# A mixer of two Mamba passes on one core: ScalarE scales the projected rows, VectorE adds them in one piece, and the queues of a unit are put in another order

## The chip, the core and the metric

The kernel runs on one core of a Trainium2 chip. The core has five engines that work from queues of their own: TensorE (PE, matrix products and transposes, results in PSUM), VectorE (DVE), ScalarE (ACT), GpSimd (POOL) and SyncE (SP, which here only starts DMAs). An engine takes its instructions strictly in the order in which they stand in its queue. An instruction that needs the result of another engine waits for a semaphore, and everything behind it in that queue waits too. The metric is the device time of one launch in microseconds (us), lower is better.

## What is computed

Input is x of shape (8, 32, 32, 128) in float32: 8 sequences of 1024 tokens with 128 channels. Layer 0 is a group norm with attention. Layer 1 adds the mixer to the tokens, and then a spectral filter. The change lies in the mixer:

```python
def _mamba3(x, in_proj, conv_w, conv_b, A_log, dt_bias, D, norm_w, out_proj):
    zxbcdt = x @ in_proj
    z, xbc, dt = jnp.split(zxbcdt, [D_INNER, D_INNER + CONV_DIM], axis=-1)
    xp = jnp.pad(xbc, ((0, 0), (K - 1, 0), (0, 0)))
    conv = sum((xp[:, i:i + l, :] * conv_w[:, i] for i in range(K))) + conv_b
    xbc = jax.nn.silu(conv)
    xh, Bm, Cm = jnp.split(xbc, [D_INNER, D_INNER + D_STATE], axis=-1)
    dt = jax.nn.softplus(dt + dt_bias)
    A = -jnp.exp(A_log)
    y = _ssd(xh, dt, A, Bm, Cm) + xh * D[None, None, :, None]
    yg = y.reshape(b, l, D_INNER) * jax.nn.silu(z)
    yn = yg * jax.lax.rsqrt(jnp.mean(yg * yg, -1, keepdims=True) + EPS) * norm_w
    return yn @ out_proj
...
t = t + _L1_attn_ref(_ln_t(t), ...)   # forward pass + pass over the reversed tokens
```

D_INNER is 256 (four heads of 64), D_STATE 64, K = 4 taps. `_ssd` works in chunks of 64 tokens: inside a chunk, C B^T is multiplied by a triangle of decays exp(segsum) and applied to x dt; each chunk also leaves a state, the states are passed on from chunk to chunk with a decay, and C, weighed with the decay since the chunk's start, reads them.

## The kernel before, in words

**Units.** The mixer works on 16 units (b, d): sequence b = 0 to 7, direction d = 0 (forward) and d = 1 (backward, on the same layout with mirrored taps and triangles). One turn of the loop at L1187 is one unit, some 36 us; two make a sequence. The loop overlaps three units: while unit `u` has its scan, `following` is projected and convolved, and `last` is gated, normed and projected out. `after_it`, two units ahead, only gets its decays. `fresh` is the next sequence, whose normed tokens are turned (`turn_tokens`) and whose step sizes (softplus, `steps`) are computed while d = 0 runs.

**Order.** No scheduler chooses here: `tc.manual_schedule` (L1152) keeps the instructions of every engine in the order in which the Python code issues them. So the order of the calls in the loop is the order of all queues.

**Names of a unit**, by what the profile calls them:

- `cums`, `dsum`, `cs`, `rest`, `dec`: cumulated log decays and what is made of them (`add_decays` L792, `turn_decays` L807, `take_decays` L813, which also sends them through memory, `cd`, so that rows come back spread over partitions as `lm` and `ec`).
- `lm`: from a row of cumulated decays to the triangle of a chunk: GpSimd subtracts (`from_row`, L846), ScalarE takes relu and then exp of minus it in two halves each (`between`, L852), VectorE multiplies by `gm` (`weigh_decays`, L1034 with the operation on L1038, called C's weighing below, since `gm` is C B^T). `ec`: GpSimd multiplies by C (`weigh_start`, L857).
- `pp`, `xp`, `xs`: x projected (PSUM), copied with a pad (ScalarE, `copy_x`), convolved per half of 128 channels: one tap with the bias on ScalarE (`first_tap`, L893), three taps on VectorE (`convolve`, L901), silu on ScalarE (`activate_x`, L906).
- `pz`, `zs`: the gate projected, and its silu (L914). `pb`, `bt`, `ct`: B and C, projected and convolved at once by TensorE (L923), and their silu.
- `sx`, `xdt`, `xdd`: x turned by TensorE (L952) and multiplied by dt (L955), then by the decay to the chunk's end (`decayed_x`).
- `sb`, `bg` = (`bk`, `gm`): B turned, and C B^T (L969), copied by ScalarE; `gm` then gets its triangle mask.
- `pst`, `state`, `moved`: the chunks' states (`chunk_states`, L990) and their passing on, 29 VectorE instructions (`pass_states`, L1007, the "states" of the text below).
- `sy`: eight steps of output products in two halves (`outputs`, L1042).
- `y`: `sy` plus D x (`add_x`, L1072), times `zs` (`gate`, L1087, which also squares into `zs`, L1090).
- `misc`, `sums`, `rms_v`, `rms`: sums of the squares over channels on TensorE (`square_sums`, L1109), copied, turned (`turn_sums`, L1123), scaled by VectorE (L1125) and raised to the power -1/2 by GpSimd (L1127).
- `spo`: `y` times the output weights (`project_out`), 128 tokens by 128 channels for each of eight blocks j. `add_up` (L1131) does X[j] = spo[j] * rms[j] + X[j], eight times. After d = 1, X goes out to memory (`xd`) and comes back in another layout (`reload`, L1140) for the spectral stage.

**Buffers that tie the units.** The tags `spo`, `misc`, `pst` and `sy` come from one PSUM pool (`ps_s`), `sx`, `sb`, `px`, `pp`, `pz`, `pb`, `pd` and `pdec` from another (`ps_w`). Each pool has two buffers, handed out in turn in the order of the calls. A new tile waits until the readers of the one in its place are done. So the first of the two tiles of `pst` waits for whoever reads `spo`.

**Two orders written by hand** in addition: `behind` puts `from_row` and `weigh_start`, both on GpSimd, after a chosen VectorE instruction (the last tap of a half so far).

**Norm of later sequences.** In d = 1 the layer norm of sequence b + 2 is taken: `normalize` (L442, statistics on VectorE, power on GpSimd) and `normalized` (eight ScalarE instructions `ln_x`, L458, in two groups of four).

## Time and profile before

| what | us |
|---|---|
| three runs | 1492.85, 1494.98, 1498.38 |
| profiled execution: its run, its span | 1490.8, 1489.0 |
| granted TensorE clock in it | 0.974 |

Busy time of each engine in stretches of the profiled span:

| stretch, us | what runs | PE | DVE | ACT | POOL |
|---|---|---|---|---|---|
| 0 to 465 | attention | 438.68 | 366.44 | 297.33 | 237.31 |
| 465 to 610 | mixer, b = 0 and 1 | 125.62 | 113.95 | 96.42 | 42.62 |
| 683 to 757 | b = 3 | 66.77 | 61.21 | 49.57 | 23.46 |
| 757 to 828 | b = 4 | 65.07 | 60.72 | 49.05 | 23.21 |
| 828 to 900 | b = 5 | 65.37 | 61.45 | 49.99 | 23.63 |
| 900 to 964 | b = 6 | 57.36 | 55.00 | 42.95 | 20.70 |
| 964 to 1042 | b = 7 | 66.02 | 59.38 | 45.29 | 24.00 |
| 1042 to 1165 | end of the mixer, spectral part | 102.60 | 63.08 | 48.79 | 64.47 |
| 1165 to 1430 | spectral part | 259.11 | 197.07 | 148.35 | 32.97 |
| 1430 to 1489 | end | 39.37 | 25.01 | 1.33 | 0 |

The stretches of the mixer are cut at round times near the units' borders, so they aren't equally long. A good mark of a unit is the copy of its first state (L1013): these stand at 500.16, 538.02, 574.40, 610.03, 646.39, 682.72, 719.22, 756.71, 793.29, 828.21, 864.55, 899.76, 936.25, 973.75, 1008.42 and 1040.82 us. Their distance is what a unit costs. The last addition to X begins at 1067.52 and the spectral part's first copy at 1069.83.

How to read the lines of instructions further on: start in us, duration in us, engine, line of the code, operation, output and inputs by their names, shape, x how many instructions the line stands for, and in brackets the idle time of the engine just before it, with the engine, tile and line that ended it. "issue" is idle time in which the engine waited for nothing that the profile shows. In a row of a group (it begins with the line and engine) the two numbers behind the bar are the busy time and the mean ns of one. In a row of a window come: its borders, length, busy time of PE, PE's weight load, DVE, ACT and POOL with the number of instructions, the granted clock, the DMAs' busy share and GB/s.

### The profile page before, as it was taken

To read this page: it belongs to the slowest core of one execution; us is meant where nothing else is said; L and a number is where in the kernel's file an instruction comes from. 1 tells how busy PE (TensorE), PEld (TensorE's weight loads), DVE (VectorE), ACT (ScalarE), POOL (GpSimd) and SP (SyncE) were. 2 spreads that over 40 slices of the span, in tenths; PEclk is the share of its full clock that TensorE was granted. 3 is DMA by queue.
4 is the path that set the end of the run, shared out by engine and by line. 5 is a ranking of instruction groups with operands and counts; after the bars stand their busy time and mean duration, and the time that the engine had idled before them with its cause. 6 is when DMAs were issued, how large, how long until landed. Compare 5 with 4: busy or idle time off the path is not lost.

```text
span 1489.0 us, 45246 instructions
## 1 busy us (share of the span) xinstructions
PE 1351.5 (91%) x19782; PEld 843.7 (57%) x19782; DVE 1124.6 (76%) x2250; ACT 878.9 (59%) x1293; POOL 516.0 (35%) x510
## 2 busy tenths in 40 slices
PE   5999999999998789998989898997599899999977
PEld 2233333333334456565656566655489888899963
DVE  5688888788766788888888888877645577777745
ACT  2666666766765676767676767564255455555520
POOL 3326966876212232323232333232276111111100
PEclk8999999999999999999999999999899999999989
DMA  7101111110002334343424343431259322322258
GB/s 183 31 1 30 43 36 36 50 50 8 8 1 58 76 77 112 77 108 75 109 66 112 78 106 72 101 72 43 71 171 243 105 68 67 88 72 75 68 150 310
DMA packets 139383, 123.09 MB, mean 83 GB/s; under 512 B 44809, under 2 KB 118153, under 8 KB 135081
## 3 DMA queue, kind: packets, MB, share of 16 engines
q1 hardware_dynamic: 137064, 115.93, 30.3%
q10 hardware_dynamic: 2112, 4.19, 0.7%
q8 instruction: 157, 2.57, 0.7%
q14 instruction: 50, 0.40, 0.1%
HBM read 78.15 MB, written 34.08 MB: 75 GB/s over the span
## 4 chain that ended last, share of the span: by engine, by line
PE 60%; DVE 14%; issue 10%; ACT 9%; POOL 4%; DMA 2%; DVEq 0%; SPq 0%; ACTq 0%; POOLq 0%
PE pg L1407 10%; PE pt L626 9%; PE py L1441 8%; PE po L647 7%; DVE state L1016 4%; PE pd L667 4%; PE sy L1064 3%; PE pb L923 2%; POOL ec L859 2%; PE pf L1325 2%; PE pz L868 2%; ACT ln_x L458 2%; POOL rms L1127 1%; DVE y L1078 1%; PE pz L1520 1%
## 5 line engine op out<-in xcount | busy, mean ns | idle before, releaser
L631 ACT ACTIVATE pr<-pt 128x1024 f32<-128x1024 f32 x256 | 248.0, 1021 | 117.3 <-PE pt L626 115.9
L656 DVE TENSOR_TENSOR two<-pr,pr 128x1024 f32<-128x1024 f32 x128 | 162.8, 1312 | 19.4 <-ACT pr L631 18.5
L1418 DVE COPY gs<-pg 128x512 f32<-128x512 f32 x256 | 158.8, 684 | 19.8 <-PE pg L1407 15.1
L1420 ACT COPY gs<-pg 128x512 f32<-128x512 f32 x256 | 132.7, 604 | 68.9 <-PE pg L1407 53.1
L626 PE MATMUL pt<-q,k 32*128 32x512 f32 x1024 | 160.7, 658 | 7.0 <-ACT pr L631 4.5
L1407 PE MATMUL pg<-taps,mst 32*128 32x128 f32 x4096 | 148.3, 283 | 6.7 <-ACT gs L1420 3.1
L1407 PEld LDWEIGHTS pg<-taps,mst 32*128 32x128 f32 x4096 | 135.0, 190 | 20.2 <-issue 14.7
L647 PE MATMUL po<-pr,v 128*32 128x512 f32 x1024 | 141.1, 609 | 0.0
L901 DVE SCALAR_TENSOR_TENSOR xs<-xp,cw,xs 128x1024 f32<-128x1024 f32 x96 | 123.1, 1283 | 16.3 <-ACT xs L893 12.8
L859 POOL TENSOR_TENSOR ec<-ec,ct 128x2048 f32<-128x2048 f32 x16 | 72.7, 4541 | 163.5 <-issue 104.0
L1441 PE MATMUL py<-gs,u 128*32 128x128 f32 (+1 forms) x4096 | 127.8, 277 | 0.0
L923 PE MATMUL pb<-bxt,wbc 128*128 128x512 f32 x256 | 117.3, 612 | 7.2 <-ACT zs L914 7.2
L1441 PEld LDWEIGHTS py<-gs,u 128*32 128x32 f32 (+1 forms) x4096 | 112.0, 141 | 7.2
L1127 POOL TENSOR_TENSOR rms<-rms_v,mhalf 128x8 f32<-128x8 f32 x16 | 39.5, 2466 | 206.8 <-DVE rms_v L1125 206.8
L1430 POOL TENSOR_SCALAR u<-u 128x512 f32<-128x512 f32 x16 | 23.9, 1496 | 231.1 <-DMA u<-ud 158.9
L626 PEld LDWEIGHTS pt<-q,k 32*128 32x128 f32 x1024 | 47.7, 188 | 86.6 <-issue 33.5
L1016 DVE SCALAR_TENSOR_TENSOR state<-state,dec,pst 128x64 f32<-128x64 f32 x448 | 87.4, 275 | 1.3
L923 PEld LDWEIGHTS pb<-bxt,wbc 128*128 128x128 f32 x256 | 48.3, 193 | 66.2 <-issue 57.9
L1064 PE MATMUL sy<-lm,xdt 64*64 64x64 f32 x2048 | 67.5, 227 | 16.8 <-DVE lm L1038 9.5
L1064 PEld LDWEIGHTS sy<-lm,xdt 64*64 64x64 f32 x2048 | 62.2, 137 | 28.3 <-issue 28.1
L647 PEld LDWEIGHTS po<-pr,v 128*32 128x32 f32 x1024 | 28.1, 110 | 88.4 <-issue 84.5
L458 ACT ACTIVATE ln_x<-X,b_shift,ln_r 128x128 f32<-128x128 f32 x128 | 51.8, 481 | 37.2 <-DVE b_shift L453 37.2
(277 smaller groups left out, 2771.2 us busy)
## 6 DMA issues: line engine op xcount, KB each, us to landing
lm<-cd SPq DMA_DIRECT2D x32, 512.0 KB
ec<-cd SPq DMA_DIRECT2D x32, 512.0 KB
ud<-sp SPq DMA_DIRECT2D x8, 1024.0 KB
u<-ud SPq DMA_DIRECT2D x32, 256.0 KB
yd<-sums SPq DMA_DIRECT2D x32, 256.0 KB
moved<-state SPq DMA_DIRECT2D x48, 128.0 KB
yt<-yd SPq DMA_DIRECT2D x6, 1024.0 KB
X<-in_x SPq DMA_DIRECT2D x8, 512.0 KB
```

The lines of the kernel that those rows point to most:

```text
L626: nc.tensor.matmul(pt[:, i, :], lhsT=k[rows, j * P : (j + 1) * P], rhs=q[rows, cols], start=True, stop=True)
L631: nc.scalar.activation(pr[:, 2 * g : 2 * g + 2, :].rearrange("p i t -> p (i t)"), pt.rearrange("p i t -> p (i t)"), AF.Exp, scale=SCALE,)
L647: nc.tensor.matmul(po[rows, :], lhsT=vs[b][:, j, rows], rhs=pr[:, h, :], start=(j == 0), stop=(j == NT - 1))
L656: nc.vector.tensor_tensor(two, sums["pr"][:, 2 * g : 2 * g + 2, :], pr[:, 2 * g : 2 * g + 2, :], ALU.add)
L901: u.convolved = nc.vector.scalar_tensor_tensor(acc, xp[:, at : at + T], cw[u.d][:, n, i : i + 1], acc, ALU.mult, ALU.add)
L923: nc.tensor.matmul(u.pb[:, i * 512 : (i + 1) * 512], lhsT=wbc[u.d][:, k, :], rhs=xt[:, at : at + 512], start=(k == 0), stop=(k == KC - 1),)
L1016: nc.vector.scalar_tensor_tensor(u.state[:, k, h, :], u.state[:, k - 1, h, :], u.dec[:, c, h, j : j + 1], u.pst[c][:, j, h, :], ALU.mult, ...
L1064: nc.tensor.matmul(u.py[c][h * HP : (h + 1) * HP, r, j, :], lhsT=left, rhs=right, start=(kind == 0), stop=(kind == 1 or k is None),)
L1407: nc.tensor.matmul(pts[g][:, e, :], lhsT=mst[rows, n * 4 + e, :], rhs=taps[rows, cols].rearrange("p f q m i -> p (f q m i)"), start=True, ...
L1418: nc.vector.tensor_copy(to, frm)
L1420: nc.scalar.copy(to, frm)
L1441: nc.tensor.matmul(py[t * 32 : t * 32 + 32 - 16 * m, q // 2, :], lhsT=u[:, i, m:, :, :, q * FC + f].rearrange("p k b i -> p (k b i)"), rhs ...
```

## The change

- `add_up` is replaced by two steps. `scale_rows`: eight ScalarE activations (Identity with a per-row scale `rms`) from `spo` into the first half of `y`. `add_rows`: one VectorE addition of the 128x1024 result to X, at the end of the unit, behind the second half of the outputs. The store of X follows it; `reload` comes one unit later (`stored`).
- `turn_x` comes before `add_x(last)`: the turned x and `xdt` stand ahead of `y` on VectorE.
- `between(u, Exp)` comes right after `take_decays`, ahead of `bg` on ScalarE, for both directions.
- Both gates, and so both squares, come before the second half of x is projected and copied; `first_tap(following, 0)` comes after `end(last)` instead of before the gates, `first_tap(following, 1)` after the gate's projections.
- `add_decays(after_it)` of d = 1 comes before `decayed_x`, `turn_decays` of it right after `end(last)`.
- `weigh_decays(u, 0)` comes right after `decayed_x`, the second half before the taps of `following`; both stood after `pass_states`.
- `end` has the sums turned between blocks 4 to 5 and 6 to 7 of `spo`, instead of behind the taps of `following`.
- Taps 0 and 1 of half 0 stay before the states, tap 2 and silu of half 0 go behind them. So `from_row` and `weigh_start` follow other instructions.
- In `steps`, `sp_u` (1 + exp) comes after the pause in the generator, so that `weigh_decays(u, 1)` and two taps stand ahead of it.
- In `normalize`, the power on GpSimd may be issued later than the statistics, and is then put behind a tap of `following`.

The arithmetic stays the same apart from where the product with `rms` is rounded.

```diff
@@ -124,10 +124,12 @@
     mhalf = filled("mhalf", [P, 1], -0.5)
     quarter = filled("quarter", [P, 1], 0.25)
+    begun = []
+
     def rsqrt(pool, src, n, scale, eps, name):
         t = pool.tile([P, n], F32, tag=name + "_v", name=name + "_v")
-        nc.gpsimd.tensor_scalar(t, src, scale, eps, ALU.mult, ALU.add)
+        begun.append(nc.gpsimd.tensor_scalar(t, src, scale, eps, ALU.mult, ALU.add))
         r = pool.tile([P, n], F32, tag=name, name=name)
         nc.gpsimd.tensor_tensor(r, t, mhalf.to_broadcast([P, n]), ALU.pow)
         return r
@@ -439,14 +441,14 @@
         nc.vector.tensor_reduce(far[0:1, 0:1], pf, AX.X, ALU.add)
         nc.vector.tensor_copy(bad, far[0:1, 0:1])
-    def normalize(pool, b):
+    def normalize(pool, b, later=False):
         st = pool.tile([P, NT, 6], F32, tag="ln_st", name=f"b_st{b}")
         mv = pool.tile([P, NT, 2], F32, tag="ln_mv", name=f"b_mv{b}")
         for j in range(NT):
             nc.vector.bn_stats(st[:, j, :], X[b][:, j, :])
         for j in range(NT):
             nc.vector.bn_aggr(mv[:, j, :], st[:, j, :])
-        return mv, rsqrt(pool, mv[:, :, 1], NT, 1.0, 1e-5, "ln_r")
+        return mv, None if later else rsqrt(pool, mv[:, :, 1], NT, 1.0, 1e-5, "ln_r")
     def normalized(b, pool, mv, rstd, wide=None):
         shift = pool.tile([P, NT], F32, tag="ln_s", name=f"b_shift{b}")
@@ -501,9 +503,9 @@
         nc.vector.tensor_scalar(e, v, -1.0, None, ALU.mult)
         nc.vector.tensor_tensor(e, e, v, ALU.min)
         nc.scalar.activation(e, e, AF.Exp)
+        yield
         u = small("sp_u")
         nc.vector.tensor_scalar(u, e, 1.0, None, ALU.add)
-        yield
         lg = small("sp_l")
         nc.scalar.activation(lg, u, AF.Ln)
         yield
@@ -1089,10 +1091,10 @@
             nc.vector.tensor_tensor(u.y[:, n, :], u.y[:, n, :], u.zs[:, n, :], ALU.mult)
             nc.scalar.activation(u.zs[:, n, :], u.y[:, n, :], AF.Square)
-        def project_out(u, half):
-            if half == 0:
+        def project_out(u, js):
+            if js[0] == 0:
                 u.po = wide_psum(ps_s, f"spo{u.tag}").rearrange("p (j e) -> p j e", j=NT)
-            for j in range(4 * half, 4 * half + 4):
+            for j in js:
                 for n in range(2):
                     nc.tensor.matmul(
                         u.po[:, j, :],
@@ -1128,12 +1130,15 @@
                 u.rstd, v.rearrange("p q k -> p (q k)"), mhalf.to_broadcast([P, NT]), ALU.pow
             )
-        def add_up(u):
+        def scale_rows(u):
+
+            u.rows = u.y[:, 0, :].rearrange("p (j c) -> p j c", j=NT)
+            for j in range(NT):
+                nc.scalar.activation(u.rows[:, j, :], u.po[:, j, :], AF.Identity, scale=u.rstd[:, j : j + 1])
+
+        def add_rows(u):
             x = X[u.b]
-            for j in range(NT):
-                nc.vector.scalar_tensor_tensor(
-                    x[:, j, :], u.po[:, j, :], u.rstd[:, j : j + 1], x[:, j, :], ALU.mult, ALU.add
-                )
+            nc.vector.tensor_tensor(x, x, u.rows, ALU.add)
             if u.d == 1:
                 nc.sync.dma_start(xd[u.b].rearrange("(j p) c -> p j c", p=P), x)
@@ -1159,10 +1164,12 @@
         def end(u):
-            project_out(u, 0)
-            u.misc = wide_psum(ps_s, f"misc{u.tag}")
-            square_sums(u, u.misc)
-            project_out(u, 1)
+            project_out(u, range(4))
+            misc = wide_psum(ps_s, f"misc{u.tag}")
+            square_sums(u, misc)
+            project_out(u, range(4, 6))
+            turn_sums(u, misc)
+            project_out(u, range(6, 8))
         add_decays(first)
         turn_decays(first)
@@ -1183,80 +1190,83 @@
         activate_bc(first)
         compare_denominators(most, least, wide_psum(ps_w, "pf")[0:1, :2])
-        last = None
+        last = stored = None
         for at, u in enumerate(units):
             following = units[at + 1] if at + 1 < len(units) else None
             after_it = units[at + 2] if at + 2 < len(units) else None
             fresh = u.b + 1 if u.d == 0 and u.b + 1 < B else 0
+            early_decays = after_it and u.d == 1
             if following and u.d == 1:
                 turn_decays(following)
             if at == 0:
                 between(u, AF.Relu, 1.0)
             if following:
                 take_decays(following)
+            between(u, AF.Exp, -1.0)
+            turn_x(u)
+            weigh_start(u, u.convolved)
             if last:
                 add_x(last)
-            turn_x(u)
-            weigh_start(u, u.convolved)
             turn_b(u)
             if fresh:
                 turn_tokens(fresh, seqs[fresh], wide_psum(ps_w, f"px{fresh}"))
             if following:
-                take_x(following, 0)
+                project_x(following, 0)
+                copy_x(following, 0)
             if last:
                 gate(last, 0)
+                gate(last, 1)
             if following:
                 project_x(following, 1)
-            if last:
-                gate(last, 1)
-            if following:
                 copy_x(following, 1)
+            if early_decays:
+                add_decays(after_it)
             decayed_x(u)
+            weigh_decays(u, 0)
             if last:
                 end(last)
+            if early_decays:
+                turn_decays(after_it)
             if following:
-                first_tap(following, 1)
-                convolve(following, 0, range(pad - 1))
+                first_tap(following, 0)
             if last:
-                turn_sums(last, last.misc)
-            early_decays = after_it and u.d == 1
-            if early_decays:
-                add_decays(after_it)
-            else:
-                between(u, AF.Exp, -1.0)
-            if following:
-                convolve(following, 0, range(pad - 1, pad))
+                scale_rows(last)
+            b = u.b + 2 if following else 0
+            norm = None
+            if u.d == 1 and b < B:
+                norm = normalize(bridge, b, later=True)
             going = iter(())
             if fresh:
                 going = steps(fresh, seqs[fresh], wide_psum(ps_w, f"pd{fresh}"))
                 next(going)
-                next(going)
-            project_z(u, 0)
-            if early_decays:
-                turn_decays(after_it)
-                between(u, AF.Exp, -1.0)
-            activate_z(u, 0)
-            project_z(u, 1)
-            activate_z(u, 1)
+            weigh_decays(u, 1)
             if following:
-                activate_x(following, 0)
-            if last:
-                add_up(last)
+                convolve(following, 0, range(pad - 1))
             next(going, None)
-            b = u.b + 2 if following else 0
-            norm = normalize(bridge, b) if u.d == 1 and b < B else None
+            for n in range(2):
+                project_z(u, n)
+                activate_z(u, n)
+            if following:
+                first_tap(following, 1)
+            if norm:
+                mv = norm[0]
+                norm = mv, rsqrt(bridge, mv[:, :, 1], NT, 1.0, 1e-5, "ln_r")
+                if following:
+                    behind(begun[-1], following.convolved, "beside the states")
             if following:
                 from_row(following, following.convolved)
             chunk_states(u)
             pass_states(u)
+            next(going, None)
             norming = normalized(b, bridge, *norm) if norm else iter(())
             next(norming, None)
-            if last and last.d == 1:
-                reload(last)
-            weigh_decays(u, 0)
-            weigh_decays(u, 1)
+            if stored:
+                reload(stored)
+            stored = None
             if following:
+                convolve(following, 0, range(pad - 1, pad))
+                activate_x(following, 0)
                 between(following, AF.Relu, 1.0)
                 project_bc(following)
                 activate_bc(following)
@@ -1268,13 +1278,16 @@
                 activate_x(following, 1)
             next(norming, None)
             outputs(u, 1)
+            if last:
+                add_rows(last)
+                stored = last if last.d else None
             last = u
         add_x(last)
         for n in range(2):
             gate(last, n)
         end(last)
-        turn_sums(last, last.misc)
-        add_up(last)
+        scale_rows(last)
+        add_rows(last)
         reload(last)
     early.close()
```

## The prediction

> **What bounds the kernel now.** I read the page's busy shares first, then a window of one sequence in the mixer, then the instructions in order of time on each engine in that window.
>
> ```profile
> PE 1351.5 (91%) x19782; PEld 843.7 (57%) x19782; DVE 1124.6 (76%) x2250; ACT 878.9 (59%) x1293; POOL 516.0 (35%) x510
> ```
>
> TensorE is busy 91% over all, but the change touches only the mixer (about 478 to 1070 us), so the stretch to read is one sequence there, two units (d = 0 and d = 1):
>
> ```profile
> 610.00:683.00 73.00, 65.50 (x990) 43.85 (x990) 61.33 (x140) 49.86 (x72) 23.66 (x16) 1.00 0.38 88
> ```
>
> Of 73.00 us TensorE is busy 65.50, VectorE 61.33, ScalarE 49.86. Neither of the first two is full: they wait for one another in turn. The gain open to any new order is what TensorE idles, some 7 us a sequence. TensorE's own lines say for whom it waits (start, duration, last the idle time and its releaser):
>
> ```profile
> 610.37 7.11 PE L923 MATMUL pb<-bxt,wbc 128*128 128x512 f32 x16 [0.44 <-ACT zs L914]
> ...
> 623.26 1.86 PE L952 MATMUL sx<-ident,xs 128*128 128x128 f32 x15 [0.53 <-ACT xs L906]
> 626.36 1.15 PE L969 MATMUL sb<-ident,bt 64*64 64x64 f32 x32 [1.25 <-DVE xdt L955]
> ...
> 635.81 0.64 PE L1109 MATMUL misc<-zs,ones 128*32 128x256 f32 x8 [0.20 <-ACT zs L1090]
> ```
> ```profile
> 664.25 1.15 PE L969 MATMUL sb<-ident,bt 64*64 64x64 f32 x32 [1.87 <-DVE xdt L955]
> ...
> 672.52 0.64 PE L1109 MATMUL misc<-zs,ones 128*32 128x256 f32 x8 [0.20 <-ACT zs L1090]
> ...
> 678.74 1.99 PE L868 MATMUL pz<-bxt,win 128*128 128x512 f32 x4 [0.28 <-ACT cs L811]
> ```
>
> With 0.40 before sy (653.64, for C's weighing L1038), 0.43 before the second pb (683.07) and 0.3 inside pst (643.81 to 646.11, where 1.98 is its length, for the X sums L1134) these waits make 0.44 + 0.53 + 1.25 + 0.20 + 0.30 + 0.40 + 1.87 + 0.20 + 0.28 + 0.43 = 5.90 us. The other 1.95 us (0.78 and 1.17, both inside sy) have the releaser "issue": nothing that the change moves ends them, and I leave them.
>
> VectorE and GpSimd:
>
> ```profile
> 639.11 0.17 DVE L1125 TENSOR_SCALAR rms_v<-misc 128x8 f32<-128x8 f32 x1 [2.54 <-PE misc L1123]
> ...
> 642.00 2.16 DVE L1134 SCALAR_TENSOR_TENSOR X<-spo,rms,X 128x128 f32<-128x128 f32 x8 [0.39 <-POOL rms L1127]
> ```
> ```profile
> 493.42 3.62 POOL L846 TENSOR_TENSOR lm<-cs,lm 128x2048 f32<-128x2048 f32 x1 [8.88 <-DVE xs L901]
> ...
> 1034.92 1.63 POOL L1127 TENSOR_TENSOR rms<-rms_v,mhalf 128x8 f32<-128x8 f32 x1 [9.60 <-DVE rms_v L1125]
> ```
> ```profile
> 493.51 3.58 DVE L501 TENSOR_SCALAR sp_e<-sp_v 128x64 f32<-128x64 f32 x1
> ```
>
> **The Trainium skill.** "SBUF — State Buffer", section "Who interferes with whom", says that VectorE and GpSimd share a port pair: a VectorE operation with two SBUF inputs, or a one-source one in a two-port mode (tensor_scalar among them), and a GpSimd operation that reads SBUF shut each other out; the first to start holds it. The trace agrees: sp_e (0.20 us elsewhere) took 3.58 from 493.51 because L846 had begun at 493.42. The power rms takes 1.63 alone and 2.54 at the median, where a tap ran first. "ScalarE: Activation LUTs", section "What ACT_TABLE_LOAD costs", prices a per-row pointer operand at about 93 ns and the overlap of neighbouring activations at about 93 ns. The rows below agree.
>
> ```profile
> L458 ACT ACTIVATE ln_x<-X,b_shift,ln_r 128x128 f32<-128x128 f32 x128 | 51.8, 481 | 37.2 <-DVE b_shift L453 37.2
> ...
> L893 ACT ACTIVATE xs<-xp,cb,cw 128x1024 f32<-128x1024 f32 x32 | 39.8, 1242 | 0.6
> L906 ACT ACTIVATE xs<-xs 128x1024 f32<-128x1024 f32 x32 | 33.9, 1058 | 13.8 <-DVE xs L901 13.7
> ...
> L1456 ACT COPY half<-py 128x128 f32<-128x128 f32 x64 | 17.0, 265 | 66.0 <-ACT gs L1420 36.1 <-issue 22.1 <-PE py L1441 7.9
> ```
>
> L893 has two pointers where L906 has none: 184 ns more, 92 each. Eight ln_x in a row take 3.19 us, 0.39 apart, so 0.09 of 0.481 overlap.
>
> **The change, part by part.** I walk the queues of one sequence with these durations, start to start: tap 1.27; 128x1024 tensor_tensor 1.13; y 0.66; states 5.7; silu 0.97; relu or exp of half lm 0.95; bg, bxt 1.0; bt and ct together 2.78; table 1.29; sx 0.95 a half; sb 2.0; px 1.15; pp or pz 1.8 each; spo 1.87 for eight products' half; pst 1.98; pb 7.05; a hand-over of about 0.14 (0.18 from TensorE).
>
> *Scaled rows.* Removed: eight L1134, 2.08 us on VectorE. Added: one 128x1024 addition, 1.13 us, after the last tap, hidden while TensorE finishes sy. Added on ScalarE: eight 128x128 activations from PSUM with one pointer: L1456's 265 + 92 - 93 overlap = 0.27 us, 2.2 together. Bounds: 0.20 (nothing for the pointer) to 0.39 (ln_x's spacing). I take 0.27. They stand before zs in ScalarE's queue, and pst waits for them instead of L1134.
>
> *xdt before y.* xdt's first half now follows half of sx at once: 0.95 + 0.18 + 1.13 + 0.14 = 2.40 against sx's 1.90, so sb waits 0.50 instead of 1.25 and 1.87. Gain 2.1 a sequence.
>
> *Squares before the second xp copy, C weighed early, decays added before spo, pst no longer behind L1134.* The waits 0.20, 0.20, 0.40 and 0.28 go, as the work now ends over 0.5 us ahead. pst's 0.30 becomes 0.18 in d = 1: first_tap ends, 8 x 0.27 = 2.2 follow, while spo's last quarter and pz (4.6) run. Gain 1.2.
>
> *Exp of lm moved ahead of bg.* Where ln_x's second half lies in front (d = 0), ScalarE needs from silu to bg's end 1.56 + 1.29 + 0.69 + 1.91 + 1.0 = 6.45, plus 0.14. TensorE reaches pp after 0.14 + 0.95 + 0.18 + 1.13 + 0.14 + 2.0 + 1.15 = 5.69. New wait 0.90; none in d = 1, where bg waits for sb as before.
>
> *sp_u (L505) behind two taps and one weighing (d = 0).* From the end of pd: 0.18, softplus head 0.68, weighing 1.13, taps 2.54, sp_u 0.18, 0.14, then on ScalarE ln 0.27, table 1.29, zs 0.92, 0.14 = 7.5. TensorE has pz 3.6 and pst 2.0 meanwhile, so pb waits 1.9, where it waited for nothing here. In d = 1 the wait for zs stays at some 0.23 (0.43).
>
> *Last tap of half 0 behind the states, so silu of half 0 stands between ln_x and relu.* In d = 1, from the states' start: 5.7 + 0.2 + 1.56 + 0.97 + 1.90 + 2.78 + 0.97 + 0.14 = 14.2 until sx may start; TensorE is there after 0.17 + 7.05 + 5.4 = 12.6. Wait 1.56 instead of 0.53. In d = 0 it just fits.
>
> Sum of waits after: 0.50 + 0.50 + 0.90 + 1.89 + 0.23 + 0.18 + 1.56 = 5.76, against 5.90. Per sequence -0.1; over six, -0.8.
>
> *Ends of the mixer.* In unit 0 sp_e is no longer behind L846. bg ends at 486.9 (two exps later), pp 490.6, pd 492.3, pz 495.9, pst 497.9: the states start 2.2 us before the old 500.16. In (6,1) and (7,0) nothing but one weighing and two taps (3.7 us, all two-input) follows rms_v on VectorE, so the power has to wait for all three instead of one; pst of the next steps slips by about 1.5 each, +3. At the very end 2.2 + 1.1 replace 2.16, less two of spo's rows: +0.6. DMAs: the xd store leaves at the unit's end, before the cd store, whose exps come 4 us later; reload goes one unit later, past the moved copies and well before the transform. Both cost nothing: SP's queue is waiting there anyway.
>
> Total: -0.8 - 2.2 + 3 + 0.6 = +0.6 us on the profiled span of 1489.0. The runs shown have 1490.8 to 1498.4 with median 1494.98; I forecast **1495 us**, no change. About 0.5% (7.5 us) is what a measurement of this kernel can tell from no change.
>
> **Rivals.**
> - *Faster.* The removed waits (3.3 us a sequence) are all plain, the added ones (c. 3.2: bg, zs, silu) are small differences of long ScalarE chains. If these chains run half a microsecond shorter each, or the issue gaps of sy fall into the new waits, half of the gain stays: 1.7 x 7 = 12 us: 1483. For it: VectorE ends with 2 to 3 us of slack in each unit. Against: ScalarE's busy time rises to about 54 of 72.
> - *Slower by ScalarE's queue.* If the eight activations cost ln_x's 0.39, d = 1 gains 1.0 us of wait on pst, and both last units too: +8, 1503; with 0.5, +15.
> - *Slower by the port.* sp_u is a tensor_scalar directly behind the tap that releases L846's operation. If L846 gets the port first, sp_u is held 3.6 us, and ln, zs and pb with it: 7 x 3.4 = +24, 1519. It decides when sp_e's exponential ends after the second tap (now 2.6 us before it), or if the hand-over to GpSimd beats the next VectorE issue; at 640.39 sp_v followed a tap without a gap and L846 began 0.08 after its tap, so I doubt it.
> - *Not what it says*: the queues are kept in written order, so it is done.
>
> **Numbers.** Forecast 0.45, faster 0.30, ScalarE's queue 0.15, port 0.10. So faster 0.30, same 0.45, slower 0.25. Range 1482 to 1513: the likeliest alone 1488 to 1502, the rest takes in 12 us to the fast side and ScalarE at 0.5; the port's case is left out.
>
> **What would show it.** sb's wait near 0.5; L1134 gone, eight activations 0.27 apart; pb waiting near 1.9 for zs in d = 0; sx waiting 1.5 for silu in d = 1; sp_u 0.2 long. It is wrong if sp_u shows 3.6, if a sequence in mid-mixer is not 71 to 74 us, or if pst waits over 1 us for the scaled rows.

## The result, and the profile after

The changed kernel takes 1474.16 us (median of four runs, 1471.66 to 1474.91), the kernel before on the same chip 1496.49: a ratio of 0.9851, interval 0.9827 to 0.9875. The forecast was no change, 1495 us in 1482 to 1513. The kernel became faster by 22 us, and the time lies outside the range.

The profiled spans are 1489.0 and 1469.9 us, 19.1 apart. Cut at marks that both traces have, the difference lies here (us; "first state" is the copy L1013, now L1015):

| stretch | before | after | difference | forecast |
|---|---|---|---|---|
| start to the mixer's first sx | 477.43 | 474.26 | -3.17 | 0 |
| first sx to unit 0's first state | 22.73 | 20.95 | -1.78 | -2.2 |
| unit 0 to unit 12 (six sequences) | 436.09 | 431.58 | -4.51 | -0.8 |
| unit 12 to unit 15 | 104.57 | 103.10 | -1.47 | +3 |
| unit 15 to the end of the last addition to X | 28.86 | 29.58 | +0.72 | +0.6 |
| from there to the end | 419.32 | 410.43 | -8.89 | 0 |

The first row is an execution's own scatter: the instructions there are the same in every kernel below, and the mark stood between 471.4 and 479.3 us in their profiles. The largest row is the last one, behind the mixer, where the change touches nothing.

The page's busy times of the kernel after:

```profile
PE 1340.2 (91%) x19782; PEld 841.3 (57%) x19782; DVE 1095.4 (75%) x2138; ACT 912.9 (62%) x1421; POOL 505.9 (34%) x510
```

VectorE has 29 us less to do: 16 of them are the sums, and 11 are `sp_e` and `sp_u`, which GpSimd's `from_row` no longer holds up. ScalarE has 34 us more, the scalings. TensorE's instructions are the same in number, yet it is busy 11 us less: 3.4 of these lie in the mixer and 3.1 in the spectral part's main loop. Kernel before, from unit 0 to 15 and then in the stretch of pg and py (the spectral part's main loop):

```profile
500.16:1040.82 540.66, 485.24 (x7372) 324.53 (x7372) 449.14 (x1020) 359.82 (x499) 168.39 (x96) 0.99 0.37 84
...
1163.44:1437.10 273.66, 267.77 (x8192) 247.00 (x8192) 199.82 (x444) 149.42 (x319) 32.97 (x32) 0.99 0.28 74
```

Kernel after, the same two stretches:

```profile
495.21:1029.89 534.68, 481.84 (x7372) 326.32 (x7372) 425.06 (x918) 391.55 (x619) 162.09 (x99) 0.99 0.37 84
...
1151.23:1419.63 268.40, 264.67 (x8192) 245.24 (x8192) 200.07 (x444) 149.28 (x319) 33.03 (x32) 0.99 0.29 75
```

Instruction for instruction the second stretch is the same, and it is 5.3 us shorter.

TensorE's waits in the mixer, in order of time (a d = 1 unit's states at 674.22, then the turn of a d = 0 unit):

```profile
674.49 7.11 PE L925 MATMUL pb<-bxt,wbc 128*128 128x512 f32 x16 [0.37 <-ACT zs L916]
686.72 0.27 PE L1066 MATMUL sy<-lm,xdt 64*64 64x64 f32 x1 [1.82 <-issue]
688.40 1.86 PE L954 MATMUL sx<-ident,xs 128*128 128x128 f32 x15 [0.57 <-ACT xs L908]
690.70 1.15 PE L971 MATMUL sb<-ident,bt 64*64 64x64 f32 x32 [0.44 <-DVE xdt L957]
695.11 3.71 PE L870 MATMUL pp<-bxt,win 128*128 128x512 f32 x8 [1.30 <-ACT bg L979]
708.96 1.98 PE L1001 MATMUL pst<-xdd,bg 64*64 64x128 f32 x64
712.67 7.14 PE L925 MATMUL pb<-bxt,wbc 128*128 128x512 f32 x16 [1.74 <-ACT zs L916]
```

Nearly every wait has the size that the prediction gave it: sb 0.44 (forecast 0.50), pb for zs 1.74 in d = 0 (1.9) and 0.37 in d = 1 (0.23), pp for bg 1.30 here and 0.53 a sequence earlier (0.90). So have the new instructions:

```profile
704.93 2.18 ACT L1137 ACTIVATE y<-spo,rms 128x128 f32<-128x128 f32 x8 [1.75 <-POOL rms L1129]
```
```profile
709.80 0.19 DVE L508 TENSOR_SCALAR sp_u<-sp_e 128x64 f32<-128x64 f32 x1
```

Eight scalings 0.27 apart, and sp_u 0.19 long. Both of the rivals that ended slower are gone with these two lines. One thing does not fit the sum: the distance of the first states. In before it goes from 34.9 to 37.5 us between units 1 and 13, with no order in it. In after it is 35.17, 36.75, 35.17, 36.75, 35.17, 36.75, 35.16, 36.75, 35.17, 36.76, 35.17, 36.81, though TensorE's "issue" times in these units lie anywhere between 0 and 2.45.

### The profile page after: what moved, and what is told of

It is laid out like the page before. It is cut to its first block, busy times and chain, and to the rows that moved or that the text cites. A ratio compares the mean times of both kernels' runs of the same rounds, so it can differ in the third digit from the quotient of the medians.

```text
span 1469.9 us, 45286 instructions
## 1 busy us (share of the span) xinstructions
PE 1340.2 (91%) x19782; PEld 841.3 (57%) x19782; DVE 1095.4 (75%) x2138; ACT 912.9 (62%) x1421; POOL 505.9 (34%) x510
## 3 DMA queue, kind: packets, MB, share of 16 engines
q8 instruction: 157, 2.57, 0.7%
## 5 line engine op out<-in xcount | busy, mean ns | idle before, releaser
L1420 PE MATMUL pg<-taps,mst 32*128 32x128 f32 x4096 | 145.2, 280 | 4.4 <-ACT gs L1433 3.5
L1420 PEld LDWEIGHTS pg<-taps,mst 32*128 32x128 f32 x4096 | 133.3, 188 | 16.4 <-issue 11.4
L628 PEld LDWEIGHTS pt<-q,k 32*128 32x128 f32 x1024 | 47.6, 186 | 85.5 <-issue 32.3
L1129 POOL TENSOR_TENSOR rms<-rms_v,mhalf 128x8 f32<-128x8 f32 x16 | 27.9, 1742 | 187.5 <-DVE rms_v L1127 187.5
L848 POOL TENSOR_TENSOR lm<-cs,lm 128x2048 f32<-128x2048 f32 x16 | 57.9, 3621 | 60.6 <-DVE sp_u L508 30.8
L1099 PE MATMUL spo<-wo,y 128*128 128x128 f32 x512 | 71.0, 288 | 7.9 <-DVE y L1091 7.8
L957 DVE TENSOR_TENSOR xdt<-sx,dt 128x1024 f32<-128x1024 f32 x32 | 37.9, 1220 | 52.9 <-PE sx L954 52.9
```

The lines of the kernel that those rows point to most:

```text
L628: nc.tensor.matmul(pt[:, i, :], lhsT=k[rows, j * P : (j + 1) * P], rhs=q[rows, cols], start=True, stop=True)
L1420: nc.tensor.matmul(pts[g][:, e, :], lhsT=mst[rows, n * 4 + e, :], rhs=taps[rows, cols].rearrange("p f q m i -> p (f q m i)"), start=True, ...
```

## The experiments

### Behind the mixer: the place of the instructions in the stream

In pg and py each round, from one group of py to the next, takes 4.11 us. In before, some rounds take up to 4.98, with TensorE idle for nothing that the profile shows. TensorE in before:

```profile
1213.86 2.01 PE L1441 MATMUL py<-gs,u 128*32 128x128 f32 x64
1215.80 0.82 PE L1407 MATMUL pg<-taps,mst 32*128 32x128 f32 x17
1217.08 1.62 PE L1407 MATMUL pg<-taps,mst 32*128 32x128 f32 x47 [0.46 <-issue]
1218.63 2.02 PE L1441 MATMUL py<-gs,u 128*32 128x128 f32 x64
1220.58 2.23 PE L1407 MATMUL pg<-taps,mst 32*128 32x128 f32 x64
1222.74 2.01 PE L1441 MATMUL py<-gs,u 128*32 128x128 f32 x64
```

From py at 1213.86 to py at 1218.63 are 4.77 us, to the next one 4.11. The kernel after runs 4.11 through nearly all rounds:

```profile
1196.79 2.01 PE L1454 MATMUL py<-gs,u 128*32 128x128 f32 x64
1198.73 2.23 PE L1420 MATMUL pg<-taps,mst 32*128 32x128 f32 x64
1200.90 2.01 PE L1454 MATMUL py<-gs,u 128*32 128x128 f32 x64
```

To move TensorE's instructions without changing their work, matmuls that nothing reads were put ahead of the last unit's outputs, where TensorE waits anyway:

```diff
+            if not following:
+                idle = wide_psum(ps_w, "idle")
+                for _ in range(16):    # 16, 32, 48 or 64
+                    nc.tensor.matmul(idle[:32, 0:1], lhsT=ones[:, :32], rhs=ones[:, 0:1], start=True, stop=True)
             outputs(u, 0)
```

With 16 and 64 in the kernel before, and 64 in the kernel after:

> The kernel before, with 16 matmuls of one column that nothing reads, on TensorE ahead of the last unit's outputs, where it idles 7.2 us for the weighing. Between the last addition to X and the end the profiled span went from 419.3 us (before) to 410.4 (after), though the change touches nothing there; 5.3 of it lie in the stretch of pg and py, where six or more idle times of TensorE named 'issue' are gone. Theory A: these idle times depend on where TensorE's instructions stand in its stream, and the change moved them by the number of its waits. Then 16 idle matmuls move them too: this stretch changes by 2 us or more, probably towards 268.4 from 273.7, and the run is 3 to 9 us from the kernel before. Rival B: the gain comes from what the mixer leaves behind (a buffer that is free earlier, a transfer that starts earlier). Then nothing moves: 273.7 within 0.5 us, the run within 2 us of before. In both the mixer stays as it was.

> As with 16, but 64 idle matmuls in the kernel before (some 3 us, inside the 7.2 us wait). Theory A: the stretch of pg and py (273.7 us) changes by 2 us or more, by another amount than with 16. Rival B: 273.7 within 0.5 us, the run within 2 us of before.

> The changed kernel with 64 idle matmuls ahead of the last unit's outputs, where TensorE waits 5.7 us for the states. Theory A: its stretch of pg and py (268.4 us, nearly free of 'issue') becomes longer, by 1 to 6 us, and the run with it. Rival B: 268.4 within 0.5 us and the run within 2 us of the changed kernel, 1474.

With 48 in the kernel after, once these were known:

> The changed kernel with 48 idle matmuls ahead of the last unit's outputs. In the runs so far TensorE's idle times in pg and py fell on the same rounds of that loop in before and with 64 matmuls added (rounds 4 to 24), and on other rounds with 16 added (29 to 53); with 64 added to the changed kernel its stretch stayed at 268.4 us. So the pattern seems to repeat every 64 matmuls, and the changed kernel, whose TensorE queue holds 32 more waits than before, to stand where 16 more matmuls put the kernel before. Theory A (place in the stream): 48 more bring the changed kernel to where before stands: idle times on rounds 4 to 24, the stretch 272 to 274 us, the run 4 to 6 us over the changed kernel. Rival B (what the mixer leaves behind): 268.4 within 0.7, the run within 2 us.

And the offsets that were left:

> The kernel before with 32 idle matmuls ahead of the last unit's outputs. In the trace each idle matmul is two matmuls and two weight loads, so 64 are 256 instructions, and the page says that TensorE's instructions come in packets of 16.4 KB (157 packets, 2.57 MB), 252 of its matmuls and loads each: 64 idle matmuls are one packet, which is why they changed nothing, and 16 are a quarter of one. If the changed kernel stands 16 behind before, 32 added here put it where 16 added put the changed kernel. Place in the stream: the stretch of pg and py of both agrees within 1 us, and its idle times fall on the same rounds. Rival: the two stretches differ by over 2 us, and the place doesn't explain the difference between the two kernels.

> As above with 48 (three quarters of a packet): the place of the changed kernel with 32. Place in the stream: the stretch agrees with that one's within 1 us. Rival: over 2 us apart.

> The changed kernel with 16 idle matmuls: the place of before with 32. Place in the stream: stretch within 1 us of that one's, and the run over the changed kernel's by as much as the stretch is over 268.4. The mixer from unit 0 to 15 stays at 534.5 to 534.8, since its units don't follow TensorE's idle times.

> The changed kernel with 32 idle matmuls: the place of before with 48. Place in the stream: stretch within 1 us of that one's. Rival: over 2 us apart. Mixer 534.5 to 534.8 in both cases.

Measured: the stretch of pg and py in the profile, the rounds of it that took over 0.12 us longer (the first is 0; in a range it is some of them), and the ratio of the runs to before:

| idle matmuls | before: stretch, rounds | ratio (interval) | after: stretch, rounds | ratio (interval) |
|---|---|---|---|---|
| 0 | 273.66, 4 to 24 and 43 | 1 | 268.40, 53 | 0.9851 (0.9827 to 0.9875) |
| 16 | 269.01, 29 to 53 | 0.9970 (0.9952 to 0.9987) | 269.87, 9 to 37 | 0.9894 (0.9866 to 0.9922) |
| 32 | 268.83, 5 to 21, 43, 52 | 0.9976 (0.9963 to 0.9989) | 268.79, 36 to 57 | 0.9907 (0.9878 to 0.9937) |
| 48 | 272.98, 8 to 56 | 0.9994 (0.9976 to 1.0012) | 276.58, 4 to 50 | 0.9906 (0.9876 to 0.9937) |
| 64 | 273.45, 4 to 20 and 43 | 1.0006 (0.9984 to 1.0028) | 268.36, 49 and 53 | 0.9888 (0.9854 to 0.9921) |

Three things follow. First, the place matters: with 48 idle matmuls the kernel after loses 8.2 us in a stretch whose work and whose surroundings are the same. Rival B expected 0.7 at most. Second, 64 change next to nothing in either kernel: the stretch stays within 0.3 us, on nearly the same rounds. This went against the expectation. The page gives the reason for the number (the line of the DMA queue that carries TensorE's instructions: packets, MB, share):

```profile
q8 instruction: 157, 2.57, 0.7%
```

In the trace an idle matmul is two matmuls and two weight loads, so 64 are 256 instructions. A packet holds 2.57 MB / 157 = 16.4 KB, and 2 x 19782 / 157 = 252 of TensorE's matmuls and loads, to which its waits come. With 32 or more idle matmuls the page counts 158 packets. 64 idle matmuls are one packet, and the pattern comes back after one packet.

Third, the place can be counted, and it is one scale for both kernels. Take TensorE's instructions in the trace (matmuls, weight loads and its waits) in the order of their starts, counted from 0. The first matmul of pg is number 23185 in before and 23208 in after. The change moved it by 23 instructions, as many as TensorE has more waits up to there (155 instead of 132); an idle matmul moves it by 4. What is left of this number after division by 256 is the place in a packet:

| place | 17 | 40 | 81 | 104 | 145 | 168 | 209 | 232 |
|---|---|---|---|---|---|---|---|---|
| kernel, idle matmuls | before, 32 | after, 32 | before, 48 | after, 48 | before, 0 and 64 | after, 0 and 64 | before, 16 | after, 16 |
| stretch, us | 268.83 | 268.79 | 272.98 | 276.58 | 273.66, 273.45 | 268.40, 268.36 | 269.01 | 269.87 |

The stretch is slow from 81 to 145 and fast at the other places. Before stands at the end of the slow part, after just behind it. The expectations had taken the change for a shift of 16 idle matmuls, 64 instructions, and so compared different places. The further kernels below fit: five made from after, at 161 or 168, took 268.2 to 269.5 us, and one made from before, at 145, took 274.5. The two with a product of pb doubled, at 17 and 40, were slower than their places say (270.05 and 271.97), so the place is not all of it.

The idle times named "issue" show what happens at such a place. From unit 0's first state to the end of py the 18 profiles of this document have 257 of them over 0.15 us. All 257 stand ahead of an instruction whose number leaves 193 or 194 after division by 256, and 249 end 1.1 to 1.7 us after a packet of q8 has ended. So in these places TensorE waits for the next packet of its own instructions. Why it waits for some packets and not for others stays open.

What the change does to this stretch beyond its place is nothing that these runs can tell: over the four places of each kernel (0, 16, 32, 48) the mean is 271.12 us in before and 270.91 in after, with 268 to 277 us at single places. Not all of the 5.3 us is place, though. In the first pair TensorE's clock stood at 0.5 for 6.8 us of this stretch in before and for 3.4 us in after, which is worth about 1.7 us (see below); the place has the other 3.6. Of the rest behind the mixer, the way from the last addition to pg's first matmul took 93.76, 92.54, 94.16 and 93.81 in before and 91.76, 91.92, 91.60 and 91.98 in after: 1.8 us that no place takes away. The spectral part's first transposes wait for the buffer of spo. In before, VectorE's additions free it:

```profile
1069.83 1.94 PE L1320 MATMUL cpt<-ident,ln_x 128*128 128x128 f32 x8 [4.33 <-DVE X L1134]
```

In after, ScalarE's scaling does, and they start at 1058.27, 1.2 us before the addition to X ends at 1059.47 (in before they start 0.15 us after its end):

```profile
1058.27 1.09 PE L1333 MATMUL cpt<-ident,ln_x 128*128 128x128 f32 x8 [3.36 <-ACT y L1137]
```

In the run further down that puts the sums back on VectorE, the transposes start 0.14 us after the end of the addition again, and the way is 92.91 us, 1.1 more than the mean of after (91.8).

The same ten profiles give the mixer's own scatter. From unit 0 to 12 before took 436.09, 436.76, 441.61, 440.33 and 440.22 us (mean 439.0), all with the same instructions; after took 431.58, 431.47, 431.47, 431.43 and 431.59. So the mixer's gain was 7.5 us in these six sequences as a mean, more than the first pair of profiles shows.

Two things scatter in before. Its "issue" times in these units are 9.6, 11.7, 12.6, 12.9 and 14.0 us. And the clock record shows 0.5 instead of 1.0 for 3.4 us at a time, which happened 2, 1, 4, 3 and 2 times; such a dip, at half speed, costs TensorE about 1.7 us. Less both, before takes 423.1, 423.4, 422.2, 422.3 and 422.8 us: it pays for both in full. The kernel after has 9.4 to 10.6 us of "issue" and two or three dips in the same units, the dips all in the 36.75 half of a sequence, and pays for neither. One unit with a dip and without (before and its run with 16 idle matmuls, then after and its run with 16):

```profile
719.22:756.71 37.49, 33.95 (x492) 22.06 (x491) 30.19 (x75) 21.46 (x32) 7.18 (x5) 0.95 0.39 90
714.50:750.22 35.72, 32.33 (x492) 21.17 (x491) 30.08 (x74) 21.46 (x32) 7.18 (x5) 1.00 0.41 95
...
602.30:639.05 36.75, 33.83 (x498) 23.57 (x498) 27.82 (x56) 27.73 (x46) 12.14 (x9) 0.95 0.38 88
607.60:644.34 36.74, 32.37 (x498) 22.26 (x498) 27.72 (x56) 27.70 (x46) 12.13 (x9) 1.00 0.38 88
```

The mixer from unit 0 to 15 with 16 and 32 idle matmuls in the kernel after was 537.04 and 537.05 instead of 534.5 to 534.8. The excess is in the last three units, where the granted clock was 0.95 against 0.98 in the kernel after, and not in units 0 to 12. The start of the mixer follows the clock too: from the first sx to unit 0's first state before took 22.7 us in all five profiles, and after 20.95 in three of them, but 24.34 with 16 and 32 idle matmuls, where pp and pz took 5.40 us each in dips instead of 3.71.

The runs as a whole are less sharp. The mean ratio over the four places is 0.9985 for before and 0.9890 for after, so that an estimate of the change at an average place is 1 - 0.9890 / 0.9985 = 1.0%, some 14 us. The other 8 of the 22 us are not the place of pg and py alone: with 16 and 32 idle matmuls the profiles of after lose 3.4 us in the mixer's start and 2.5 in its last units, and only 1.5 and 0.4 in pg and py. The kernel after with 64 idle matmuls, at the same place as with none, was measured at 0.9888 against 0.9851, so this division is good to a few us only.

### What sets the units of the changed kernel

The first edit takes away the largest wait that the change had added:

```diff
-            if following:
-                convolve(following, 0, range(pad - 1))
             next(going, None)
+            if following:
+                convolve(following, 0, range(pad - 1))
```

> The changed kernel with sp_u (one plus the exponential) issued after the weighing but ahead of the two taps, so that the logarithm, the table and the silu of the gate come about 1.5 us earlier in d = 0. The wait of pb for zs (1.74 us in each d = 0) should fall to 0.3. The prediction counted this wait as 1.9 us on the path of each sequence: then a sequence falls from 71.92 to 70.2, and the run is 10 us faster. Theory now: the distance of the units in the changed kernel is the same to 0.05 us in every sequence whatever TensorE's idle times are, so a loop through ScalarE sets it (states, silu, relu, B and C, exponentials, copy of bg, then TensorE to pst), and this wait lies beside it: the sequence stays at 71.9 within 0.4, the run within 3 us of the changed kernel.

The wait went from 1.74 to 0.28 us. Nothing was gained: 1478.06 us, ratio 0.9898 (0.9861 to 0.9935), 4 us over the changed kernel where within 3 was expected. Most units kept 35.17 and 36.75; three of them became 0.8 to 1.1 us longer (36.01, 36.24, 36.19), so that units 0 to 15 took 537.94 instead of 534.68. These three, all of the 35.17 half, have no "issue" time; the clock was 0.953 in them, and TensorE was busy 33.5 to 34.1 us instead of 32.3 to 32.5. So the wait was on nobody's path.

The loop that sets the units can be read off ScalarE in the kernel after (start, duration; the states begin at 674.22 and end just before 680):

```profile
680.12 1.65 ACT L460 ACTIVATE ln_x<-X,b_shift,ln_r 128x128 f32<-128x128 f32 x4 [3.73 <-DVE b_shift L455]
681.67 1.04 ACT L908 ACTIVATE xs<-xs 128x1024 f32<-128x1024 f32 x1
682.62 1.99 ACT L857 ACTIVATE lm<-lm 128x1024 f32<-128x1024 f32 x2
...
692.01 2.01 ACT L857 ACTIVATE lm<-lm 128x1024 f32<-128x1024 f32 x2
694.04 1.01 ACT L979 COPY bg<-sb 128x1024 f32<-128x1024 f32 x1
694.95 1.02 ACT L475 COPY bxt<-px 128x1024 f32<-128x1024 f32 x1
697.13 1.01 ACT L890 COPY xp<-pp 128x1024 f32<-128x1024 f32 x1 [1.16 <-PE pp L870]
```

The states end just before 680.12, and from there to bg's end at 695.05 ScalarE has no idle time. Then TensorE goes without a wait from pp (695.11) to the end of pst (710.94), and the next states begin at 710.97. 5.90 + 14.93 + 15.92 = 36.75: states, ScalarE, TensorE. TensorE's idle times ahead of pp lie beside ScalarE's stretch, and whatever they are, ScalarE is later. The wait of sx for xs shows the trade: in the six units from d = 1 to d = 0, sy's "issue" and sx's wait are 1.04 + 1.29, 1.94 + 0, 1.82 + 0.57, 2.45 + 0, 0.55 + 1.88 and 2.37 + 0. The sum is 1.9 to 2.5 each time: where one is there, the other is not.

The short half (35.17) leaves ScalarE earlier. TensorE in it, from the states at 639.05 to those at 674.22:

```profile
654.20 1.86 PE L954 MATMUL sx<-ident,xs 128*128 128x128 f32 x15 [0.16 <-ACT xs L908]
656.50 1.15 PE L971 MATMUL sb<-ident,bt 64*64 64x64 f32 x32 [0.44 <-DVE xdt L957]
658.51 3.71 PE L870 MATMUL pp<-bxt,win 128*128 128x512 f32 x8
```

Here pp does not wait for bg. The loop goes from the states through ScalarE to the silu of xs, from there to sx, through xdt on VectorE to sb, and on along TensorE to pst. TensorE comes to sx only 0.16 to 0.58 us early, so in this half it is nearly as late as ScalarE.

If so, extra work on TensorE in the right place should vanish in after and not in before. The first product of pb was done twice, for both halves of the tokens (two more matmuls in each unit):

```diff
-                for k in range(KC):
+                for n, k in enumerate((0, *range(KC))):
...
-                        start=(k == 0),
-                        stop=(k == KC - 1),
+                        start=(n <= 1),
+                        stop=(n == 0 or k == KC - 1),
```

> The kernel before with the first of the four products of pb done twice, for both halves: two more 128x512 matmuls a unit, 0.89 us of TensorE, 14 us over the mixer, no other work changed. Theory: before is bound by TensorE and its idle times one after the other, so nothing absorbs this; the distance from unit 0's first state to unit 15's goes from 540.7 (541 to 546 in the runs of before with idle matmuls) to 554 or more. Rival (both kernels have a loop beside TensorE that sets the units): half of it or less.

> The changed kernel with the same two more matmuls a unit. Theory: in the changed kernel the loop from the states through ScalarE to bg and from there on TensorE to pst sets the units, and TensorE waits in pb, sx and pp beside it; up to 1.3 us a unit in d = 1 is absorbed, and in d = 0 what pb's 1.74 us wait and 0.2 to 0.6 of sx hold. The distance from unit 0 to 15 goes from 534.7 to 537 to 543, at most half of the 14 us added. Rival (TensorE bounds the changed kernel too, only with fewer waits): 548 or more.

The work added is twice what the expectations say: each of these matmuls is two in the trace, of 0.44 us each. pb in a d = 1 unit of both, where it took 7.11 us without:

```profile
694.25 8.83 PE L923 MATMUL pb<-bxt,wbc 128*128 128x512 f32 x20 [0.44 <-ACT zs L914]
```
```profile
681.39 8.83 PE L925 MATMUL pb<-bxt,wbc 128*128 128x512 f32 x20 [0.36 <-ACT zs L916]
```

That is 1.72 us a unit, 20.6 up to unit 12 and 25.8 up to unit 15. In the kernel after the distances up to unit 12 became 36.73 to 36.75 (from 36.75) in one half: all 1.72 us absorbed. In the other half, after a first 35.18, they became 35.96 to 36.23 (from 35.17), so that only 0.7 to 0.9 was absorbed. Units 0 to 15 took 540.66 (from 534.68), 6.0 us more. In the kernel before they took 561.20, 14.5 to 20.5 more than in the five profiles of before with and without idle matmuls. Up to unit 12 its "issue" times were 6.3 us (9.6 to 14.0 without the matmuls), and its clock dipped six times; less both it took 439.0 us, against 422.2 to 423.4. So before pays 16 to 17 of the 20.6 us there and hides only a small part in its idle times, while after pays 4. Both numbers lie where the theory had them (554 or more, 537 to 543), but "nothing absorbs this" is too strong for before. As whole runs the two are no evidence: 1.0056 (1.0036 to 1.0076) for before, and 0.9939 (0.9923 to 0.9956) for after against its 0.9851. These matmuls move all later instructions too, and the stretch of pg and py was 270.05 in the first and 271.97 in the second.

### The parts one by one

Only x turned ahead of y, in the kernel before:

```diff
-            if last:
-                add_x(last)
             turn_x(u)
             weigh_start(u, u.convolved)
+            if last:
+                add_x(last)
```

> The kernel before with one part of the change alone: x is turned, and xdt made, ahead of y on VectorE. The prediction counted this as 2.1 us a sequence (sb's waits of 1.25 and 1.87 become 0.50 each), some 15 us over the mixer. Theory: before is bound by TensorE, so a wait less is a gain: from unit 0's first state to unit 15's 526 to 532 us instead of 541 to 546. Rival: y comes 2.4 us later, and the gates, squares and output products that hang on it wait in its place: 538 to 546.

This one edit gives 1475.29 us, ratio 0.9863 (0.9801 to 0.9924): as much as the whole change. Units 0 to 15 took 526.42 us, 8 less than in the changed kernel, and its stretch of pg and py is one of the slow ones (274.50, long rounds 4 to 26). TensorE's waits in it:

```profile
617.77 0.27 PE L1064 MATMUL sy<-ec,state 64*64 64x64 f32 x2 [1.15 <-issue]
619.47 1.86 PE L952 MATMUL sx<-ident,xs 128*128 128x128 f32 x15 [0.17 <-ACT xs L906]
621.76 1.15 PE L969 MATMUL sb<-ident,bt 64*64 64x64 f32 x32 [0.44 <-DVE xdt L955]
631.22 0.64 PE L1109 MATMUL misc<-zs,ones 128*32 128x256 f32 x8 [0.20 <-ACT zs L1090]
```

sb waits 0.44 as it does in after, and nothing came in its place in these units: the squares wait 0.20 as before, though y is later. (In the last unit spo waits 3.15 us for y instead of 0.83.) So in the kernel before, whose TensorE is bound wait by wait, this part alone is worth about 2 us a sequence, as the prediction had it, and with the other edits added the mixer is 8 us longer again.

The same part undone in the changed kernel:

> The changed kernel with that part undone: y ahead of xdt again. sb waits 1.7 to 2.4 us instead of 0.44. Theory (loop through ScalarE): in d = 1 bg is late by 1.1 to 1.3 us because ScalarE comes to it late, so most of this is absorbed, and 36.75 becomes 36.8 to 37.3; in d = 0 sb is on the loop, and 35.17 (counted from a d = 0 unit's first state to the next is 36.75 or 35.17 by which half of the loop it holds) grows by 1 to 2: 534.7 becomes 543 to 552. Rival (the waits of TensorE add up whatever the loop): both grow alike, 553 to 560.

1478.51 us, ratio 0.9889 (0.9833 to 0.9946); units 0 to 15 took 536.06, less than expected. The long half stayed at 36.75 to 36.82, where sb's wait (up to 1.58) is absorbed by ScalarE; the short half, after a first 35.18, became 35.68 to 36.21, 0.5 to 1.0 more. Up to unit 12 that makes 435.09 us against 431.58; the last units are shorter and hide part of it. So what is worth 2 us a sequence in one kernel is worth 0.6 in the other.

The sums put back on VectorE, in the changed kernel:

```diff
-            if last:
-                scale_rows(last)
...
             next(going, None)
+            if last:
+                add_up(last)
...
-            if last:
-                add_rows(last)
-                stored = last if last.d else None
+            stored = last if last and last.d else None
```

> The changed kernel with the sums put back: no scaling on ScalarE and no addition at the unit's end, but eight fused operations on VectorE (2.1 us) behind the taps and ahead of the states, where before had them; the rest stays changed. Theory: VectorE waits only 0.7 to 1.0 us for pst there, so the states, which begin the loop that sets the units, start 1.1 to 1.4 us later in each unit: 534.7 becomes 550 to 556 from unit 0 to 15. Rival (the place of this work doesn't matter, the removed waits do): within 3 us of 534.7.

This was 1528.4 us, ratio 1.0215 (1.0161 to 1.0269), and 587.71 us from unit 0 to 15: three times the loss expected. The expectation had counted the states' start only. TensorE in it:

```profile
651.36 2.95 PE L1001 MATMUL pst<-xdd,bg 64*64 64x128 f32 x60 [2.72 <-DVE X L1136]
```

pst takes the buffer of spo, so it waits for the last of the eight additions, which VectorE begins only after the taps and sp_u (649.15), and then the states wait for pst: 2.7 to 3.1 us on the loop in each unit up to 12, some 35 of the 48 us lost there. Most of the rest fits the clock: it dipped eleven times up to unit 12, against twice in the kernel after, and nine dips more at 1.7 us each would be 15 us; no run tells the two apart. With the rest of the change in place, scaling on ScalarE is a condition, not an extra.

### The two edits that lengthen the loop

The loop begins at the states' end, and the change had put a tap and a silu behind it. The last tap and silu of half 0 were put ahead of the states again, alone and then together with sp_u ahead of the taps. The edit of both:

```diff
             weigh_decays(u, 1)
+            next(going, None)
             if following:
-                convolve(following, 0, range(pad - 1))
-            next(going, None)
+                convolve(following, 0)
...
             if following:
+                activate_x(following, 0)
                 first_tap(following, 1)
...
-                convolve(following, 0, range(pad - 1, pad))
-                activate_x(following, 0)
                 between(following, AF.Relu, 1.0)
```

(In the first of the two runs `next(going, None)`, which issues sp_u, stays behind taps 0 and 1, and the last tap follows it.)

> The changed kernel with the last tap of half 0 and its silu ahead of the states again, as in before. Theory (loop through ScalarE): the tap (1.28 us) and the silu (1.0 us) leave the stretch between the states' end and bg, and VectorE's 0.7 to 1.0 us wait for pst pays most of the tap: ScalarE's stretch is shorter by 1 us in d = 1 and up to 2 in d = 0, until pb, which waits for zs, bounds it; 534.7 becomes 523 to 531 from unit 0 to 15. Rival (TensorE's own work and its idle times named 'issue' are the floor): 533 to 538.

> Both edits on the changed kernel: last tap and silu of half 0 ahead of the states, and sp_u ahead of the taps. Theory: with pb no longer waiting 1.74 us for zs, the gain of the first is whole: 518 to 528 us from unit 0 to 15, the run 6 to 15 us under the changed kernel. Rival (TensorE is the floor, and its 'issue' times, which the wait for zs had taken up, show again): 533 to 540.

The first gave 1466.87 us, ratio 0.9813 (0.9757 to 0.9870), with 527.60 us from unit 0 to 15. Both together gave 1460.21 us, ratio 0.9763 (0.9707 to 0.9820), with 520.24 us. Both lie within what was expected of the loop and outside what the rival allowed. In pg and py the first had one long round, the second none. TensorE in the second one waits 0.36 and 0.27 us for zs, and "issue" is the largest idle time that is left:

```profile
600.99 7.11 PE L925 MATMUL pb<-bxt,wbc 128*128 128x512 f32 x16 [0.36 <-ACT zs L916]
613.65 0.21 PE L1066 MATMUL sy<-ec,moved 64*64 64x64 f32 x1 [2.62 <-issue]
637.65 7.14 PE L925 MATMUL pb<-bxt,wbc 128*128 128x512 f32 x16 [0.27 <-ACT zs L916]
```

sp_u ahead of the taps, worth nothing alone, is worth 7 us once the loop is short enough for pb to be the next limit. The units are now irregular again (33.0 to 37.3 us), as in before. This version is faster than both kernels.

## Why the prediction was wrong

**The waits: right.** The start of the mixer (-2.2, measured -1.8 where the clock did not dip in it), the end (+0.6, +0.7), the eight scalings (0.27 each), sp_u past L846 (0.19), and the waits of sb, bg and zs came out within some 0.4 us of their figures. "sp_e is no longer behind L846" held too: it took 0.20 us instead of 3.58.

**Six sequences, forecast -0.8, shown -4.5 in the first profiles and -7.5 as a mean.** The step that failed is the one on TensorE's idle times named "issue": "nothing that the change moves ends them, and I leave them". They were taken as the same cost on both sides, and with them TensorE's waits were taken as the length of a sequence on both sides. In before this is right: TensorE bounds it, and waits, "issue" times and dips of the clock add up (9.6 to 14.0 us of "issue"; less these and the dips, 422.2 to 423.4 us in all five profiles). In after the units are set by the loop through ScalarE, and these times fall into the waits that the change had made. The sum of waits (5.76 after, 5.90 before) compared two lists that don't add up in the same way. The rival "faster" had named this ("the issue gaps of sy fall into the new waits") and gave 1483.

In the first profiles the number of a sequence is nevertheless nearly right, and that is luck. 2.7 of the 4.5 us lie between units 0 and 1 (37.86 us before, 35.17 after), for which the forecast has no term. 1.7 of them are pb, which ran into a dip of the clock there in all five profiles of before and in none of after:

```profile
501.60 8.83 PE L923 MATMUL pb<-bxt,wbc 128*128 128x512 f32 x16 [4.17 <-ACT zs L914]
```
```profile
496.44 7.14 PE L925 MATMUL pb<-bxt,wbc 128*128 128x512 f32 x16 [1.26 <-ACT zs L916]
```

The other eleven units differ by 1.8 us, and before has one more dip, of 1.7, among them.

**The silu of half 0, forecast as a wait of 1.56 of sx.** It showed as 0 to 1.88, by how much "issue" had gone before it. (Its own terms, 14.22 and 12.62, make 1.60.) The price was right, its place in a sum was not: this edit and sp_u's were on a loop, and 14 us of the mixer were lost to the two, as their removal showed.

**(6,1) and (7,0), forecast +3, shown -1.5.** The step was that the power on GpSimd has to wait for all three VectorE operations behind rms_v. It took 2.48 us in both, as long as behind a single tap in before (2.54): in (6,1) the taps had to wait for their first tap, and in (7,0) it was done at 991.58, while the two taps ran from 990.00 to 992.60 at their usual 1.30 each. So it waited for the weighing that had begun (988.87 to 990.09), and neither it nor the taps show a wait for the other. For the scaled rows pst waited not at all in (6,1), 0.46 in (7,0) and not at all in (7,1); before, it had waited 1.41 in (7,0) and 0.50 in (7,1) for the additions to X, which the forecast's list left out.

**Behind the mixer, forecast 0, shown -8.9.** The largest part of the miss. The step that failed is the whole stretch put at nothing. 5.3 us lie in pg and py: some 3.6 are the place of TensorE's instructions in their packets, which the change moves by 23 without meaning to, and some 1.7 are the clock. It is luck that the change moved the place across the edge between slow and fast; no view that the prediction read gives this ahead. 2.0 us (1.8 as a mean) lie between the last addition and pg, where ScalarE frees the buffer of spo before the last addition is done: the prediction priced the end as a chain to the addition to X and did not ask who waits for spo's buffer behind it. The run with the sums back on VectorE has 1.1 us of it again; that the buffer accounts for all of the 1.8 is not shown. The other 1.6 are nothing that the change does: 51.9 and 50.3 us for the last stretch in these two profiles, 51.3 and 51.1 as means over the four places.

## What to carry to other kernels

Waits of the busiest engine add up only while that engine bounds the loop: look for the loop (a distance that doesn't scatter is its mark), and ask of each wait, removed or added, whether it lies on it. A part of a change can be worth more than the whole, so price and try the parts one by one. And a difference in a stretch that was not touched may be the place of the instructions in their stream: shift them by instructions that do nothing, over a whole packet (256 instructions here), before a gain of half a per cent is credited to the change.

## What the runs showed of the hardware

- TensorE waits for packets of its own instructions, under the name "issue": all 257 such idle times over 0.15 us in 18 profiles stand at number 193 or 194 of a round of 256 of its instructions, and 249 end 1.1 to 1.7 us after one of the 157 or 158 packets of 16.4 KB. One stretch of 8192 matmuls took 268.4 to 276.6 us by a shift of up to 192 instructions, and was the same again after 256.
- TensorE's clock record falls to 0.5 for 3.4 us at a time. A unit with such a dip took 37.49 us instead of 35.72 where TensorE bounds the loop, and 36.75 instead of 36.74 where a loop beside it does.
- The mixer of one kernel took 540.7 to 546.7 us in five profiles where TensorE bounds it, and 534.5 to 534.8 in three of the kernel where a loop beside TensorE does (537.0 in two with a lower clock in the last units).
- The power on GpSimd took 2.48 us though one to three two-input operations of VectorE followed it: in these cases it waited for the operation that had begun, not for the queue behind it.
